# GpSimd's memsets between scatters: one of 192 floats behind each, or three of 336 behind two of thirteen

## The chip, the cores and the metric

One core of one Trainium2 chip. The metric is the time on the device in microseconds, median of several runs; lower is better. The engines are TensorE (PE in the profile, PEld for its weight loads), VectorE (DVE), ScalarE (ACT), GpSimd (POOL) and SyncE (SP). Transfers are issued from the queues of SyncE, ScalarE and GpSimd.

## The reference

A layer of a graph network: 6250 nodes with 64 features, 206,250 edges with 64 features.

```python
msg = concat([x[dst], edge_attr], axis=1)            # 206250 x 128
h = relu(msg @ W1a.T + b1a) @ W1b.T + b1b
sums = segment_sum(h, src, 6250)                     # counts likewise
agg = sums / max(counts, 1)[:, None]
z = relu(concat([x, agg], axis=1) @ W2a.T + b2a) @ W2b.T + b2b
out = layernorm(x + concat([z, x], axis=1) @ Wr.T + br)
```

The edges are ordered by `dst`; the sum is over `src`, whose values are spread over all nodes.

## The kernel before

`fast_path` does the work; `general_path` is taken only for inputs that it can't handle, and isn't run here. The edges are padded and cut into 124 blocks (`k`) of 13 tiles (`j`) of 128 edges. The bins of the sum are 49 groups of 128 nodes.

For each block:

- SyncE loads the block's edge features into `rhs` (L698, four buffers), the places of its `dst` nodes (L914), and the window of 64 node rows that they can lie in (L919).
- VectorE turns the places into a one-hot matrix below the features (`columns`, L931), and counts the edges of each bin (`bins_of`, L833 to L840); TensorE completes the counts (`counts_of`, L853 and L854), and VectorE makes of them the row in DRAM to which each edge goes (`slots`, L870 and L875).
- TensorE multiplies `rhs` by the first layer's weights (`hidden`, L951, two matmuls for each tile of edges), 4, 3, 3 and 3 tiles at a time, and ScalarE writes the relu of each part to the row buffer `orow` (L952). There are five such buffers. ScalarE also copies the node's place in its bin into each row (L1186). This copy is the first write to a buffer and waits until the 13 scatters that used the buffer five blocks earlier have landed.
- GpSimd scatters the 13 tiles (`scatter`, L958): 128 rows of 520 bytes each, to `rows` in DRAM, sorted by bin. Behind each scatter it sets the tile `rest` to zero (L966). Nothing reads `rest`.

Rows that are complete for a bin are read back by SyncE (`read`, L1008), VectorE makes a one-hot matrix of their nodes (L1034, L1037), TensorE sums them (`summed`, L1053), and the sums are added to `part` (L1107, L1109). These reads are spread over later blocks: an epoch's rows are read from four blocks after its end. What remains after the last block is read, summed and passed through the second layer and the normalisation (L1276 on).

The order on each engine is written out by hand: the loop over `k` emits for all engines in program order, and each engine takes its instructions in that order. On GpSimd that order is scatter, memset, scatter, memset. A scatter waits for the relu of its part and for the landing of the scatter eight before it. The memsets write the same tile, and in the built program each waits for the semaphore of the memset before it; a scatter doesn't wait for a memset.

Of the kernel before, what the change touches and what calls it, by code (L numbers as in the profile page):

```python
# [8 lines left out]
F32 = mybir.dt.float32  # L9
# [8 lines left out]
P = 128  # L18
# [446 lines left out]
SPREAD = 4.8  # L465
EARLY = 14
CLEAR = 4
FAR = -1000.0


# [7 lines left out]
def fast_path(  # L478
# [34 lines left out]
    nc = tc.nc  # L513
# [73 lines left out]
    const = ctx.enter_context(tc.tile_pool(name="fconst", bufs=1))  # L587
# [88 lines left out]
    with (  # L676
# [10 lines left out]
        slp = by_slot.enter_context(tc.tile_pool(name="slot", bufs=2))  # L687
        slp1 = by_slot.enter_context(tc.tile_pool(name="slot1", bufs=1))

        rest = const.tile([P, 192], F32, name="rest")  # L690
        orows = [op.tile([P, BLK, W], F32, name=f"orow{i}") for i in range(ROWS)]
        for r in orows:
            nc.gpsimd.memset(r[:, :, H], 1.0)
# [260 lines left out]
        def scatter(ep_, k):  # L954
            e, orow = epochs.index(ep_), orows[k % ROWS]
            for j in range(BLK):
                t = k * BLK + j
                s = nc.gpsimd.indirect_dma_start(  # L958
                    out=ep_.rows,
                    out_offset=bass.IndirectOffsetOnAxis(ap=rowidx[:, t : t + 1], axis=0),  # L960
                    in_=orow[:, j, :],
                    in_offset=None,
                )
                tc.declare_no_dep(s.ins, group=f"slots{e}", reason="each slot is written once")
                tc.add_to_no_dep_group(f"slots{e}", s.ins)
                nc.gpsimd.memset(rest, 0.0)  # L966
                tc.add_to_no_dep_group(f"block{k}", s.ins)
                scattered[t] = s.ins.name
                for i, st in enumerate(ep_.steps[:-1]):
                    if st.at <= k:  # L970
                        tc.declare_no_dep(s.ins, group=f"reads{i}", reason="later edges have later slots")
                if k < EARLY:
                    tc.declare_no_dep(s.ins, group="cleared", reason="no edge has these slots yet")
                if k == EARLY and j == 0:
                    for c in cleared:
                        tc.add_manual_dep(
                            s.ins, c.name,
                            mybir.DependencyInfo(mybir.DependencyClass.Sync, mybir.DependencyReason.DATA),
                            reason="edges may have these slots",
                        )  # L980
# [3 lines left out]
        def clear(e, i):  # L984

            ep_ = epochs[e]
            v = ep_.rows.rearrange("(b s) f -> b s f", b=NB)
            step = (NB - 1) // CLEAR
            parts = [(i * step, (i + 1) * step)] + [(NB - 1, NB)] * (i == CLEAR - 1)
            for b0, b1 in parts:  # L990
# [33 lines left out]
        def nodes_of(st, reads):  # L1024
# [3 lines left out]
            for b0, nb, t0, n, rt in reads:  # L1028
                node = rt[:, :, H + 1]
                if st is ep_.steps[-1] and t0 + n > ep_.low[b0]:  # L1030
# [3 lines left out]
                    nc.vector.scalar_tensor_tensor(  # L1034
                        node, ep_.unused[rest][:, at : at + nb * n], FAR, rt[:, :, H + 1], op0=ALU.mult, op1=ALU.add
                    )
# [101 lines left out]

        clears = {5 + 2 * i: (0, i) for i in range(CLEAR)}
        for e in range(1, BUFS):  # L1140
            clears.update({8 * e + 2 + 2 * i: (e, i) for i in range(CLEAR)})
        assert max(clears) < EPOCHS[0] and 5 + 2 * CLEAR <= EARLY

# [36 lines left out]
        for k, ep_ in enumerate(epoch_of):  # L1180
# [66 lines left out]
            for i in range(max(due, 1)):  # L1247
                if due > 0:
                    sum_next()
                    issue(k)  # L1250
                if i == 0 and k + 1 < NGR:
                    slots(k + 1, counts)
                if i == min(1, max(due, 1) - 1):
                    if k > 0:
                        hidden(k, ((10, 3),))
                    made.pop(k)
                    scatter(ep_, k)
# [179 lines left out]
```

## Time and profile before

| | |
|---|---|
| median of 3 runs | 2540.11 us (2535.44 to 2542.4) |
| the profiled execution | 2518.58 us |
| its span | 2516.8 us |
| mean granted TensorE clock | 0.687 |
| GpSimd busy | 2002.8 us (80%) |
| TensorE matmuls busy | 1581.3 us (63%) |
| VectorE busy | 1186.3 us (47%) |
| ScalarE busy | 331.3 us (13%) |

The profile is one execution. Each row of a group gives line, engine, operation, what is written from what is read, and the count, then busy time and the mean length of one in ns, then the engine's idle time ahead of these instructions and what ended it. "Issue" is idle time in which the engine waited for nothing that the profile shows; "remote" is a wait whose releaser it can't name. In a timeline row stand start and length in us, engine, line and operation; in brackets the idle time ahead of it. In a row of the windows stand the stretch, its length, the busy time of PE, PEld, DVE, ACT and POOL with counts, the granted clock, the mean busy share of the DMA engines, and GB/s.

### The profile page before, as it was taken

The numbers are of one execution on the slowest core, as the hardware profiler recorded it, in microseconds if no ns is written. First come the engines' busy times: TensorE is split into PE (matmuls) and PEld (weight loads), VectorE is DVE, ScalarE is ACT, GpSimd is POOL, SyncE is SP. The second block draws the span as 40 slices with busy tenths as digits, with TensorE's granted clock in tenths as the row PEclk, the third lists the DMA queues.
The fourth block names the chain that finished last, engine by engine and source line by source line (L and its number), as shares of the span: only waits on it lengthen the run. The fifth ranks groups of instructions, "written<-read, shape, count | busy, mean of one in ns | idle before, by whom it ended". The sixth has DMA issues, their size and how long they took to land.

```text
span 2516.8 us, 26639 instructions
## 1 busy us (share of the span) xinstructions
PE 1581.3 (63%) x8253; PEld 1341.0 (53%) x8253; DVE 1186.3 (47%) x1993; ACT 331.3 (13%) x807; POOL 2002.8 (80%) x3241
## 2 busy tenths in 40 slices
PE   3645543556656555565655676666766776767796
PEld 3634432444455445454444565565655565656695
DVE  5433442434344434353434454574545464546587
ACT  1211110101111111011111110111111110110115
POOL 7888888888888888888888888888878888888800
PEclk7666665656666676666666677676767676767798
DMA  6758554744454344344345454554545454446581
GB/s 165 215 178 280 157 157 119 204 116 116 116 143 133 105 133 122 111 130 116 116 118 142 128 168 145 159 167 137 165 121 167 147 176 145 151 149 182 168 259 36
DMA packets 198852, 375.33 MB, mean 149 GB/s; under 512 B 47106, under 2 KB 114037, under 8 KB 198573
## 3 DMA queue, kind: packets, MB, share of 16 engines
q1 hardware_dynamic: 121370, 223.70, 32.1%
q0 software_dynamic: 51584, 107.40, 13.4%
q10 hardware_dynamic: 25746, 42.45, 5.0%
q8 instruction: 67, 1.10, 0.2%
q14 instruction: 85, 0.69, 0.1%
HBM read 221.77 MB, written 151.59 MB: 148 GB/s over the span
## 4 chain that ended last, share of the span: by engine, by line
PE 31%; another core or an unknown queue 29%; issue 18%; DVE 10%; DMA 5%; SPq 5%; ACT 2%; ACTq 0%; DVEq 0%
PE sum_ps L1053 16%; PE h_ps L951 10%; DMA rt<-rows 3%; DVE oh L1037 2%; DVE rhs L931 2%; PE cnt_ps L853 1%; PE cnt_ps L854 1%; DVE had L840 1%; SPq L1008 1%; SPq L919 1%; DVE row L870 1%; SPq L914 1%; SPq L917 1%; PE h_ps L1162 1%
## 5 line engine op out<-in xcount | busy, mean ns | idle before, releaser
L958 POOL DMA_INDIRECT rows<-orow,rowidx x1612 | 1560.3, 968 | 390.5 <-issue 263.8
L951 PE MATMUL h_ps<-mv,rhs 128*128 128x128 f32 x3224 | 672.7, 359 | 371.6 <-issue 253.2
L1053 PE MATMUL sum_ps<-rt,oh 128*128 128x129 f32 x4006 | 720.5, 328 | 275.5 <-issue 253.3
L951 PEld LDWEIGHTS h_ps<-mv,rhs 128*128 128x128 f32 x3224 | 592.7, 263 | 462.1 <-issue 326.7
L1053 PEld LDWEIGHTS sum_ps<-rt,oh 128*128 128x128 f32 x4006 | 634.9, 235 | 346.5 <-issue 322.8
L952 ACT ACTIVATE orow<-h_ps 128x512 f32<-128x512 f32 x496 | 251.4, 518 | 2010.6 <-remote 1329.7
L966 POOL MEMSET rest<- 128x192 f32 x1612 | 443.4, 275 | 1.2
L1037 DVE TENSOR_TENSOR oh<-ramp,rt 128x512 f32<-128x512 f32 (+3 forms) x213 | 146.2, 703 | 560.8 <-DMA rt<-rows 369.4
L931 DVE TENSOR_TENSOR rhs<-rhs,ramp 64x1664 f32<-64x1664 bf16 x116 | 219.4, 1892 | 25.1 <-DMA rhs<-relt 14.2
L840 DVE TENSOR_TENSOR_SCAN had<-ramp,bins 128x700 bf16<-128x700 bf16 x124 | 200.3, 1615 | 4.2
L1109 DVE TENSOR_TENSOR part<-part,sum_ps 128x258 f32<-128x258 f32 (+2 forms) x183 | 86.1, 471 | 236.2 <-remote 160.2
L1037 DVE TENSOR_TENSOR oh<-ramp,node 128x512 f32<-128x512 f32 (+3 forms) x237 | 187.4, 791 | 8.0
L853 PE MATMUL cnt_ps<-had,one_w 128*128 128x350 bf16 x248 | 102.9, 417 | 118.5 <-issue 63.8
L870 DVE TENSOR_REDUCE row<-cnt_ps 128x14 f32<-128x700 f32 x124 | 109.0, 879 | 122.4 <-remote 98.9
L1034 DVE SCALAR_TENSOR_TENSOR node<-unused,rt 128x4 f32<-128x4 bf16 (+3 forms) x237 | 37.7, 159 | 171.6 <-DMA rt<-rows 132.3
L854 PE MATMUL cnt_ps<-bins,before_w 128*128 128x325 bf16 x248 | 104.4, 423 | 14.0 <-issue 13.2
L854 PEld LDWEIGHTS <-before_w 128*128 128x128 bf16 x248 | 29.4, 119 | 156.0 <-issue 143.2
L834 DVE TENSOR_TENSOR bins<-ramp,hi 128x650 bf16<-128x650 f32 x124 | 108.2, 873 | 0.0
L1158 DVE TENSOR_SCALAR zT<-h_ps 128x512 f32<-128x512 f32 (+1 forms) x13 | 8.6, 661 | 123.1 <-remote 107.9
L1162 PE MATMUL h_ps<-nwzz_t,zT 128*128 128x64 f32 x98 | 21.1, 385 | 63.3 <-DVE zT L1158 49.4
L1162 PEld LDWEIGHTS h_ps<-nwzz_t,zT 128*128 128x128 f32 x98 | 19.2, 291 | 65.0 <-issue 41.8
L853 PEld LDWEIGHTS <-one_w 128*128 128x128 bf16 x248 | 30.8, 124 | 30.3 <-issue 20.4
(113 smaller groups left out, 428.0 us busy)
## 6 DMA issues: line engine op xcount, KB each, us to landing
rt<-rows SPq DMA_DIRECT2D x242, 260.0 KB
rhs<-in_edgeT SPq DMA_DIRECT2D x124, 416.0 KB
rt<-rows SPq DMA_DIRECT2D x106, 390.0 KB
rows<-orow,rowidx POOLq DMA_INDIRECT x1612
rhs<-relt SPq DMA_DIRECT2D x116, 208.0 KB
rows<-padrow ACTq DMA_DIRECT2D x4, 4680.0 KB
rows<-padrow ACTq DMA_DIRECT2D x8, 2340.0 KB
rt<-rows SPq DMA_DIRECT2D x48, 325.0 KB
```

What stands on the lines that cost most here:

```text
L834: nc.vector.tensor_tensor(by_bin[:, :, 1:], ramp[:, : 2 * HALF, None].to_broadcast([P, 2 * HALF, BLK]), hi[:, None, c0 : c0 + BLK].to_broa ...
L840: nc.vector.tensor_tensor_scan(had, on, oh, 0.0, op0=ALU.mult, op1=ALU.add)
L853: nc.tensor.matmul(v, one_w, had[:, b, :], start=True, stop=False)
L854: nc.tensor.matmul(v[:, :, :BLK], before_w, oh[:, b, 1:], start=False, stop=True)
L870: nc.vector.tensor_reduce(row, v.rearrange("p i b t -> p t i b"), axis=mybir.AxisListType.XY, op=ALU.max)
L931: nc.vector.tensor_tensor(rhs[D:, :].rearrange("p (h e) -> p h e", h=2), rel, in_win[D:, :, None].to_broadcast([WIN, 2, NG * P // 2]), op= ...
L951: nc.tensor.matmul(ps[:, j, :], rhs[:, c * P : (c + 1) * P], m, start=True, stop=True)
L952: nc.scalar.activation(orow[:, k0 : k0 + n, :H], ps[:, :n, :], AF.Relu)
L958: s = nc.gpsimd.indirect_dma_start(out=ep_.rows, out_offset=bass.IndirectOffsetOnAxis(ap=rowidx[:, t : t + 1], axis=0), in_=orow[:, j, :], ...
L966: nc.gpsimd.memset(rest, 0.0)
L1037: nc.vector.tensor_tensor(res[:, at_tile : at_tile + nb * n, :], ramp[:, None, :].to_broadcast([P, nb * n, P]), node[:, :, None].to_broadc ...
L1053: nc.tensor.matmul(of_bin(b), oh[:, at_tile, :], rt[:, j * n + t, : H + 1], start=t0 + t == st.lo[b], stop=t0 + t == st.hi[b] - 1,)
```

## The change

The tile `rest` grows from 192 to 336 floats per partition. Behind the sixth and the thirteenth scatter of a block GpSimd sets all of it to zero three times; behind the other eleven it sets one float per partition to zero, once. The number of scatters, their order and their data stay the same, and so do the instructions of all other engines. The three memsets of a group write the same tile, and each waits for the semaphore of the one before it.

```diff
 CLEAR = 4
+REST = 336
+AT = (5, 12)
...
-        rest = const.tile([P, 192], F32, name="rest")
+        rest = const.tile([P, REST], F32, name="rest")
...
-                nc.gpsimd.memset(rest, 0.0)
+                for _ in range(3 if j in AT else 1):
+                    nc.gpsimd.memset(rest if j in AT else rest[:, :1], 0.0)
```

## The prediction

> **What bounds the kernel now.** I read the page first, for the busy shares and the chain that ended last; then GpSimd's groups by form and the waits; then the timeline at three places where GpSimd ran dry.
>
> ```profile
> span 2516.8 us, 26639 instructions
> PE 1581.3 (63%) x8253; PEld 1341.0 (53%) x8253; DVE 1186.3 (47%) x1993; ACT 331.3 (13%) x807; POOL 2002.8 (80%) x3241
> PE 31%; another core or an unknown queue 29%; issue 18%; DVE 10%; DMA 5%; SPq 5%; ACT 2%; ACTq 0%; DVEq 0%
> ...
> L958 POOL DMA_INDIRECT rows<-orow,rowidx x1612 | 1560.3, 968 | 390.5 <-issue 263.8 <-ACT orow L1186 64.7 <-ACT orow L952 61.4
> L966 POOL MEMSET rest<- 128x192 f32 x1612 | 443.4, 275 | 1.2
> ...
> 14.49 1.13 POOL L958 DMA_INDIRECT rows<-orow,rowidx  x1 [11.34 <-ACT orow L952]
> ...
> 2394.89 0.27 POOL L966 MEMSET rest<- 128x192 f32 x1
> ```
>
> The two GpSimd rows give busy time, mean length of one, and the idle time before them. Scatters 1560.3, memsets 443.4 and idle 390.5 + 1.2 add up to 2395 us, which is where GpSimd's last memset ends (2394.89 + 0.27 = 2395.2). So GpSimd is occupied or held from start to that point, and 121.6 us of tail follow without it. Of its idle time 263.8 us is the fixed gap ahead of a scatter (0.17 us each), and 64.7 + 61.4 = 126.1 us are waits for ScalarE's rows, 11.3 of them before the very first scatter. GpSimd alone would therefore need 2395.2 - 126.1 = 2269 us; it has 114.8 us of later waits in it, so it isn't the only bound.
>
> ```profile
> POOL rows L958 <- ACT orow L1186: 64.7, 26, 5.8
> POOL rows L958 <- ACT orow L952: 61.4, 35, 11.3
> ...
> ACT orow L952 <- remote: 1329.7, 177, 21.7
> ...
> ACT orow L1186 <- DMA rows<-orow,rowidx: 5.7, 1, 5.7
> ```
>
> The columns are total us, times, longest. ScalarE's relu L952 waits 1329.7 us for something that the profile can't name. What it needs is TensorE's products. It isn't short of row buffers: the copy L1186, the instruction that must wait until the scatters of five blocks earlier have landed, waited once, for 5.7 us. So the side of TensorE and ScalarE isn't held back by GpSimd through the buffers, and yet it is as slow as GpSimd. The timeline shows how the two are tied:
>
> ```profile
> 639.04 0.97 POOL L958 DMA_INDIRECT rows<-orow,rowidx  x1 [0.16 <-issue]
> 641.80 0.48 SPq L698 DMA_DIRECT2D rhs<-in_edgeT  x1
> 641.87 0.49 ACT L952 ACTIVATE orow<-h_ps 128x384 f32<-128x384 f32 x1 [16.06 <-remote]
> 642.64 0.97 POOL L958 DMA_INDIRECT rows<-orow,rowidx  x1 [2.36 <-ACT orow L1186]
> ...
> 1166.64 0.37 PE L951 MATMUL h_ps<-mv,rhs 128*128 128x128 f32 x1 [1.02 <-issue]
> 1167.37 0.37 PE L951 MATMUL h_ps<-mv,rhs 128*128 128x128 f32 x1 [0.36 <-issue]
> 1169.56 0.96 POOL L958 DMA_INDIRECT rows<-orow,rowidx  x1 [0.16 <-issue]
> 1170.97 0.97 POOL L958 DMA_INDIRECT rows<-orow,rowidx  x1 [0.16 <-issue]
> 1173.77 0.48 SPq L698 DMA_DIRECT2D rhs<-in_edgeT  x1
> 1173.84 0.49 ACT L952 ACTIVATE orow<-h_ps 128x384 f32<-128x384 f32 x1 [16.48 <-remote]
> 1174.60 0.97 POOL L958 DMA_INDIRECT rows<-orow,rowidx  x1 [2.40 <-ACT orow L1186]
> 1175.82 3.51 PE L1053 MATMUL sum_ps<-rt,oh 128*128 128x129 f32 x24
> ...
> 2116.30 0.96 POOL L958 DMA_INDIRECT rows<-orow,rowidx  x1 [0.16 <-issue]
> 2119.09 0.49 SPq L698 DMA_DIRECT2D rhs<-in_edgeT  x1
> 2119.16 0.49 ACT L952 ACTIVATE orow<-h_ps 128x384 f32<-128x384 f32 x1 [19.56 <-remote]
> 2119.93 0.97 POOL L958 DMA_INDIRECT rows<-orow,rowidx  x1 [2.39 <-ACT orow L1186]
> ```
>
> Scatters follow each other every 1.41 us (1169.56, 1170.97). At 1166 us TensorE starts single matmuls 0.73 us apart, with idle time that nothing explains, and ScalarE stands still for 16.48 us. Then GpSimd runs out of rows and misses a slot, and SyncE, ScalarE and TensorE all start again: 24 matmuls in 3.51 us. Had the restart nothing to do with GpSimd, the time from the last scatter to it would be scattered over anything from 0 to 20 us. It is 2.76, 2.80 and 2.79 us in the three places, after ScalarE waits of 16 to 20 us, and GpSimd's own waits are 2.36, 2.40 and 2.39 us. I read this as: an unbroken train of scatters slows TensorE's side down, and a pause in the train of somewhere between 1.4 and 2.8 us, from one scatter's start, sets it free. What carries this I can't see. Two more rows speak for it:
>
> ```profile
> 467.00:2395.00 1928.00, 1249.38 (x6399) 1059.12 (x6398) 905.43 (x1406) 215.82 (x511) 1619.69 (x2614) 0.68 0.48 140
> 2395.00:2516.80 121.80, 97.76 (x723) 87.50 (x722) 98.47 (x348) 44.72 (x133) 0.17 (x1) 0.93 0.50 150
> ```
>
> After the last scatter TensorE does 723 matmuls in 121.8 us, 5.9 per us, at a granted clock of 0.93; beside the scatters 3.3 per us at 0.68. DMA is equally busy in both (0.48 and 0.50).
>
> **The change, part by part.** It touches GpSimd's memsets only; their order among the scatters stays, no other engine's instructions move, nobody reads what they write. A block has 13 scatters, so 11 memsets of 192 floats become one float, and two become three of 336. Over 124 blocks that is 1364 short and 744 long ones in place of 1612.
>
> ```profile
> L671 POOL MEMSET padrow<- 128x780 f32 x1 | 0.7, 739 | 0.0
> masks.py:197 POOL MEMSET ident<- 128x128 f32 x1 | 0.2, 195 | 0.0
> L1419 POOL MEMSET const-float32-1.0<- 128x1 f32 x1 | 0.1, 99 | 0.0
> ...
> 0.25 0.10 POOL L1419 MEMSET const-float32-0.0<- 128x1 f32 x1 [0.25 <-issue]
> 0.28 0.10 POOL L1419 MEMSET const-float32-1.0<- 128x1 f32 x1
> ...
> 1.30 0.52 POOL L648 MEMSET rt<- 65x512 f32 x1
> 1.76 0.20 POOL masks.py:197 MEMSET ident<- 128x128 f32 x1
> ```
>
> Price of a float: (739 - 195) / (780 - 128) = 0.834 ns. From L966's 275 ns at 192 floats: one float costs 275 - 191 x 0.834 = 116 ns (99 by the row of that size), 336 floats 275 + 144 x 0.834 = 395 ns. End to end: 1364 x 0.116 + 744 x 0.395 = 158.2 + 293.9 = 452.1 us against 443.4, so +9 us. The second and third long memset of a group have no row here. Below: independent memsets overlap (0.25 and 0.28; 1.30 + 0.52 against 1.76), by some 0.06 us; 496 of these save 30 us, and the 99 ns row saves 1364 x 0.017 = 23 us more, together 9 - 53 = -44 us. Above: all write the same tile, and each waits for the semaphore of the one before. From a relu's end (2119.16 + 0.49) to the scatter that waits for it (2119.93) it takes 0.28 us; 496 x 0.28 = 139, so +148 us. I take +9, since L966's row shows 1.2 us of idle time in 1612, so GpSimd takes up a ready memset at once, and keep -44 and +148 for the range.
>
> [...] The overlap is in the rows above for tiles that don't depend on each other. [...]
>
> What the change moves is where GpSimd pauses. Behind 11 scatters the next one starts 0.97 + 0.116 + 0.17 = 1.25 us later, behind the sixth and thirteenth 0.97 + 3 x 0.395 + 0.17 = 2.32 us later. Before, no stop was longer than 1.41 us unless GpSimd ran dry. 2.32 lies inside the 1.4 to 2.8 us above. If the pause frees TensorE's side, it does so 248 times, every 6 or 7 scatters, and GpSimd runs dry less often. Waits before a block's first scatter or its eleventh are the ones that it can shorten; I count half of the 114.8 us, since 2.32 falls short of the 2.8 us seen: -57 us. This half is an estimate between none and all. Sum: +9 - 57 = -48 us. The profiled execution took 2518.58 us; 2518.6 - 48 = 2470.6. The median of the runs, 2540.11, stands 0.85% above it, so 2470.6 x 1.0085 = 2492 us. GpSimd is then the bound of the scatter stage (2278 us of its own and some 69 us of waits), and the tail's 121.6 us stay. With all waits gone and the lower price it would be 2518.6 - 115 - 44 = 2360, or 2380 us on the median's scale.
>
> The granted clock may add to it: 0.68 beside the scatters against 0.93 in the tail. [...]
>
> **The rivals.** *A, the short gaps hurt (slower).* If TensorE's side advances only in the gap between two scatters, that gap falls from 0.275 + 0.17 = 0.45 us to 0.29 us behind 11 of 13 scatters, and stalls grow between the long pauses. It decides if 2.32 us is too short to set TensorE free. Every 5% on the 1329.7 us of ScalarE's waits is 66 us: 2518.6 + 9 + 66 = 2594, or 2616 us. For it: the releases seen came at 2.76 us and later. Against it: three places only, and the next scatter needs time to take hold.
>
> *B, GpSimd gets longer.* With 0.28 us at each of 496 semaphores GpSimd needs 2269 + 148 = 2417 us without any wait, 22 us past today's 2395, and some 10 us of waits remain: 2518.6 + 32 = 2551, or 2572 us. For it: the wait is in the built instruction list. Against it: both ends are the same engine, while the 0.28 us is between two.
>
> *C, nothing comes of it.* The pauses free nothing, and TensorE's side, which doesn't wait for GpSimd's buffers, keeps its pace; then +9 us or -44 us disappear into the 114.8 us of waits: 2540 us. For it: the L1186 row. Against it: the restarts above.
>
> That the change doesn't do what it says is ruled out by the instruction list: one-float memsets behind 11 scatters, three of 336 behind the sixth and thirteenth.
>
> **How the numbers follow.** Forecast 0.54, A 0.18, B 0.16, C 0.12. About 0.3% (8 us) is what a measurement of this kernel can tell from no change, so faster 0.54, same 0.12, slower 0.34. The likeliest case's own range is 2380 to 2530; the range for 8 in 10 runs from 2410, which leaves out the extreme of full release with the lower price, to 2590, which takes in C, B and the start of A.
>
> **What would show it.** Right: L958's waits for ScalarE fall from 126 to near 70 us; L952's "remote" total falls well below 1329.7; ScalarE restarts in the pauses behind the sixth and thirteenth scatter; the long memsets follow each other 0.4 us apart. Wrong: the memsets stand 0.6 us or more apart (B); "remote" grows and GpSimd's waits with it (A); both stay (C).

## The result, and the profile after

The changed kernel took 2529.89 us (median of 13 runs, 2522.59 to 2534.48) against 2541.85 us for the kernel before in the same session (13 runs, 2535.44 to 2548.92). The medians lie 12 us apart, where 48 us were forecast. The ratio of the two, taken over all runs, is 0.9945 with a 95% interval of [0.9934, 0.9957], so the gain is about 0.5%. The profiled execution took 2527.26 us, span 2525.5 us.

GpSimd's groups by form in the profile after, then its waits and ScalarE's (total us, times, longest). The added lines shift the numbers: scatter L960, memset L969, relu L954, copy L1189, sums L1056.

```profile
L960 POOL DMA_INDIRECT rows<-orow,rowidx x1612 | 1551.4, 962 | 376.3 <-issue 324.8 <-ACT orow L954 25.3 <-ACT orow L1189 11.8
L969 POOL MEMSET rest<- 128x336 f32 x744 | 286.8, 385 | 28.7
L969 POOL MEMSET rest<- 128x1 f32 x1364 | 160.4, 118 | 0.5
...
POOL rows L960 <- issue: 324.8, 1575, 2.0
POOL rows L960 <- ACT orow L954: 25.3, 23, 3.3
POOL rows L960 <- ACT orow L1189: 11.8, 8, 2.1
...
ACT orow L954 <- remote: 1146.7, 205, 18.5
...
ACT orow L1189 <- DMA rows<-orow,rowidx: 203.4, 27, 14.8
```

GpSimd's waits for ScalarE's rows fell from 126.1 to 37.1 us, and the copy into a row buffer now waits 203.4 us for scatters to land, against 5.7 us before: in places GpSimd has become the slower side. But the gap that the profile calls "issue" rose from 263.8 to 324.8 us, and 28.7 us of idle time stand ahead of the long memsets. The timeline shows where they come from:

```profile
1008.09 0.96 POOL L960 DMA_INDIRECT rows<-orow,rowidx  x1 [0.19 <-issue]
1009.04 1.27 POOL L969 MEMSET rest<- 128x336 f32 x3
1010.67 0.97 POOL L960 DMA_INDIRECT rows<-orow,rowidx  x1 [0.36 <-issue]
1011.64 0.11 POOL L969 MEMSET rest<- 128x1 f32 x1
1011.95 0.96 POOL L960 DMA_INDIRECT rows<-orow,rowidx  x1 [0.19 <-issue]
...
1017.01 0.96 POOL L960 DMA_INDIRECT rows<-orow,rowidx  x1 [0.19 <-issue]
1017.95 1.27 POOL L969 MEMSET rest<- 128x336 f32 x3
1019.39 0.98 POOL L960 DMA_INDIRECT rows<-orow,rowidx  x1 [0.16 <-issue]
```

A one-float memset is followed by a gap of 0.19 us instead of 0.16; the first scatter of a block, behind three long memsets, comes after 0.36 us; and three memsets of 0.385 us take 1.27 us, so 0.058 us lies between two (28.7 us over 496). The stop behind the sixth scatter is 2.38 us from start to start (1017.01 to 1019.39), that behind the thirteenth 2.58 us (1008.09 to 1010.67).

The same two kernels ran once more in another session, the second of those below: 2544.95 us before, 2530.92 after, ratio 0.9945 [0.9925, 0.9965]. Its rows, before and after:

```profile
L958 POOL DMA_INDIRECT rows<-orow,rowidx x1612 | 1557.0, 966 | 421.6 <-issue 265.3 <-ACT orow L952 72.6 <-ACT orow L1186 67.8
L966 POOL MEMSET rest<- 128x192 f32 x1612 | 442.4, 274 | 1.0
```

```profile
L960 POOL DMA_INDIRECT rows<-orow,rowidx x1612 | 1547.2, 960 | 388.7 <-issue 325.1 <-ACT orow L954 30.5 <-ACT orow L1189 18.8
L969 POOL MEMSET rest<- 128x336 f32 x744 | 285.5, 384 | 28.6
L969 POOL MEMSET rest<- 128x1 f32 x1364 | 158.3, 116 | 1.0
```

Put into a ledger, which adds up to GpSimd's end, with the tail as what is left of the span:

| us | before | after | before, 2nd session | after, 2nd session |
|---|---|---|---|---|
| scatters | 1560.3 | 1551.4 | 1557.0 | 1547.2 |
| memsets | 443.4 | 447.2 | 442.4 | 443.8 |
| idle ahead of memsets | 1.2 | 29.2 | 1.0 | 29.6 |
| "issue" ahead of scatters | 263.8 | 324.8 | 265.3 | 325.1 |
| GpSimd's own total | 2268.7 | 2352.6 | 2265.7 | 2345.7 |
| other idle time ahead of scatters | 126.7 | 51.5 | 156.3 | 63.6 |
| tail | 121.4 | 121.4 | 124.5 | 119.8 |
| span | 2516.8 | 2525.5 | 2546.5 | 2529.1 |

GpSimd's own total grew by 84 and 80 us; its waits shrank by 75 and 93 us. Two large terms nearly cancel. The first pair of profiled executions even comes out 9 us slower. The profiled execution before (2518.58 us) isn't one of the 13 runs and lies 17 us under the fastest of them, and the record names no chip for it, so this pair may mix two chips. The second pair (17 us faster) is from one chip and lies near its medians (14 us faster); it is the one to go by.

### The profile page after: what moved, and what is told of

It reads as the page before. It is cut to its first block, busy times and chain, and to the rows that moved or that the text cites. A ratio compares the mean times of both kernels' runs of the same rounds, so it can differ in the third digit from the quotient of the medians.

```text
span 2525.5 us, 27135 instructions
## 1 busy us (share of the span) xinstructions
PE 1627.6 (64%) x8253; PEld 1402.9 (56%) x8253; DVE 1189.2 (47%) x1993; ACT 332.2 (13%) x807; POOL 1994.9 (79%) x3737
## 4 chain that ended last, share of the span: by engine, by line
PE 34%; another core or an unknown queue 23%; issue 17%; POOL 9%; DVE 8%; DMA 3%; SPq 3%; ACT 2%; ACTq 0%; POOLq 0%; DVEq 0%
PE sum_ps L1056 17%; PE h_ps L953 13%; POOL rows L960 7%; POOL rest L969 2%; DMA rt<-rows 2%; DVE oh L1040 2%; ACT orow L954 1%; PE cnt_ps L855 1%; PE cnt_ps L856 1%; DVE rhs L933 1%; DVE had L842 1%; SPq L1011 1%; PE h_ps L1165 1%; DVE part L1112 1%
## 5 line engine op out<-in xcount | busy, mean ns | idle before, releaser
L960 POOL DMA_INDIRECT rows<-orow,rowidx x1612 | 1551.4, 962 | 376.3 <-issue 324.8
L953 PE MATMUL h_ps<-mv,rhs 128*128 128x128 f32 x3224 | 702.6, 372 | 444.6 <-issue 240.9
L953 PEld LDWEIGHTS h_ps<-mv,rhs 128*128 128x128 f32 x3224 | 620.1, 274 | 537.9 <-issue 311.4
L1056 PE MATMUL sum_ps<-rt,oh 128*128 128x129 f32 x4006 | 728.5, 338 | 235.3 <-issue 199.8
L1056 PEld LDWEIGHTS sum_ps<-rt,oh 128*128 128x128 f32 x4006 | 662.0, 247 | 288.5 <-issue 253.1
L954 ACT ACTIVATE orow<-h_ps 128x512 f32<-128x512 f32 x496 | 250.9, 518 | 1808.4 <-remote 1146.7
L969 POOL MEMSET rest<- 128x1 f32 (+1 forms) x2108 | 447.2, 212 | 29.2
L1189 ACT CAST orow<-lo 128x13 f32<-128x13 bf16 x124 | 25.9, 209 | 220.9 <-DMA rows<-orow,rowidx 203.4
```

The source lines that it names most:

```text
L953: nc.tensor.matmul(ps[:, j, :], rhs[:, c * P : (c + 1) * P], m, start=True, stop=True)
L954: nc.scalar.activation(orow[:, k0 : k0 + n, :H], ps[:, :n, :], AF.Relu)
L960: s = nc.gpsimd.indirect_dma_start(out=ep_.rows, out_offset=bass.IndirectOffsetOnAxis(ap=rowidx[:, t : t + 1], axis=0), in_=orow[:, j, :], ...
L969: nc.gpsimd.memset(rest if j in AT else rest[:, :1], 0.0)
L1056: nc.tensor.matmul(of_bin(b), oh[:, at_tile, :], rt[:, j * n + t, : H + 1], start=t0 + t == st.lo[b], stop=t0 + t == st.hi[b] - 1,)
```

## The experiments

The kernel before does not take the same time on all chips, and neither do the others in proportion to it. In two sessions it took 2378.52 and 2378.86 us, in four others 2514.66, 2515.93, 2544.95 and 2541.85 us (the last is the session of the result). All kernels of one session share a chip, and each ratio is against the kernel before on that chip. The five sessions below ran on five different chips; for the session of the result the chip isn't on record. Each chip was used in one session only, so a property of the chip can't be told from one of the session. I call the chips of the first two quick and the others slow. Unless shown otherwise an edit is made to the changed kernel.

The theories: the **pause theory** is the prediction's (a stop in the train of scatters sets TensorE's side free). Against it stands the **pace** or **total theory**: only GpSimd's own total counts, wherever its slack stands. Rival A of the prediction (short gaps hurt) can act beside either.

### First session, a quick chip (before 2378.52 us)

**No pause**: one float behind every scatter. **One pause**: `AT = (12,)`. **Half pause**: one long memset instead of three. **Even**: 250 floats behind every scatter.

```diff
 e1_no_pause
-                for _ in range(3 if j in AT else 1):
-                    nc.gpsimd.memset(rest if j in AT else rest[:, :1], 0.0)
+                nc.gpsimd.memset(rest[:, :1], 0.0)
 e2_one_pause
-AT = (5, 12)
+AT = (12,)
 e3_half_pause
-                for _ in range(3 if j in AT else 1):
+                for _ in range(1):
 e4_even
-REST = 336
+REST = 250
...
-                for _ in range(3 if j in AT else 1):
-                    nc.gpsimd.memset(rest if j in AT else rest[:, :1], 0.0)
+                nc.gpsimd.memset(rest, 0.0)
```

> One float is set behind every scatter; no long memset is left. GpSimd's own cycle is then 1.27 us for each scatter, 2041 us over the kernel (2342 us in the changed kernel). Pause theory (an unbroken train of scatters slows TensorE's side, a stop of some 2.4 us frees it): the stops are gone, so TensorE's side falls back, GpSimd waits for rows for over 300 us in all, and the time is that of the kernel before or longer, 2540 to 2600 us. Pace theory (only GpSimd's own total counts, wherever it stops): 300 us less of its own, so 2400 to 2500 us.

> The three memsets of 336 floats stay behind the thirteenth scatter alone; one float behind the other twelve. GpSimd's own cycle is 12 x 1.27 + 2.59 = 17.8 us per block, 2205 us in all. Pause theory: half as many stops, so stalls grow up to a block's length and GpSimd's waits rise to 150 us or more; 2530 to 2560 us. Pace theory: 137 us less than the changed kernel, so 2480 to 2520 us.

> One memset of 336 floats behind the sixth and thirteenth scatter in place of three: the stop is 1.52 us from scatter to scatter in place of 2.4 to 2.6. GpSimd's own cycle is 17.0 us per block, 2104 us in all. Pause theory: 1.52 us is too short to free TensorE's side, so it comes out as with no stops, 2540 to 2600 us. Pace theory: 240 us less of its own than in the changed kernel, so 2430 to 2500 us.

> One memset of 250 floats behind every scatter: a scatter every 1.45 us, 18.9 us per block, the same own total as in the changed kernel (2342 us), spread evenly. Pause theory: no stop, so stalls of over 10 us stay, and GpSimd's longer own time comes on top of what its waits can take in: 2540 to 2590 us. Pace theory: the same total, so the changed kernel's time, about 2530 us.

Measured: no pause 2156.47 us, ratio 0.9065 [0.9053, 0.9078]; one pause 2322.61, 0.9763 [0.9750, 0.9777]; half pause 2218.57, 0.9330 [0.9318, 0.9343]; even 2454.00, 1.0319 [1.0305, 1.0334]. All the ranges that were expected, in both theories, stood on a kernel before of 2540 us, and all are missed. The differences fit the pace theory: against the changed kernel's 2462.66 us on a quick chip (fourth session) these four are 306, 140, 244 and 9 us faster, where GpSimd's own totals were expected 301, 137, 238 and 0 us shorter. ScalarE's two largest waits in the kernel without a pause:

```profile
ACT orow L1188 <- DMA rows<-orow,rowidx: 1459.0, 111, 15.4
ACT orow L954 <- PE h_ps L953: 184.3, 153, 6.8
```

No "remote" wait of the relu is left. The copy waits 1459 us for scatters to land, so TensorE's side is the full five buffers ahead at 111 of 124 blocks, with no pause in the train at all. On this chip nothing has to be set free: the pause theory fails here, and so does A.

### Second session, a slow chip (before 2544.95 us)

> The changed kernel itself, unedited, beside the kernel before in the same runs. Pace theory (where TensorE is not stalled, the time is GpSimd's own total and nothing else): the pauses cost 79 us of GpSimd's own time (2342 against 2263 us in the first pair of traces), so where the kernel before takes 2378 us the changed one takes about 2457 us, ratio 1.033. Pause theory (a stop behind the sixth and thirteenth scatter frees TensorE's side): a gain wherever it runs, ratio 0.98 to 0.995. Where the kernel before takes 2540 us again, both give 2530 us, ratio 0.995.

> The kernel before, unedited, for a trace beside the others. Where it takes 2378 us: pace theory expects that ScalarE's relu has next to no waits that the profile can't name (under 100 us against 1329.7 in the first trace) and that the copy waits for the landing of scatters of five blocks earlier instead, some 1600 us. Pause theory expects the unnamed waits of 16 to 20 us to be there still, some 1300 us in sum. Where it takes 2540 us, both expect the first trace again.

> One float behind every scatter, no pause at all. Pace theory: GpSimd's own total falls by about 225 us to 2035 us; where the kernel before takes 2378 us this takes 2157 us, ratio 0.907; where it takes 2540 us, TensorE's side is the limit and the time lies between 2300 and 2540 us, ratio 0.91 to 1.00. Pause theory: a train without a pause of over 0.29 us stalls TensorE's side more often, so where the kernel before takes 2540 us this is slower than the changed kernel, above 2530 us and up to 2616 us.

> 250 floats behind every scatter: GpSimd's own total is about that of the changed kernel (2336 against 2342 us), spread evenly, cadence 1.45 us, no pause. Pace theory: the time of the changed kernel within 0.5%: 2454 us where the kernel before takes 2378 us, ratio 1.032; about 2530 us where it takes 2540 us. Pause theory: where the kernel before takes 2540 us, this one keeps the stalls and has 73 us more of GpSimd's own time, 2580 to 2620 us, ratio 1.015 to 1.03, clearly slower than the changed kernel.

Here g3_short is the kernel without a pause, and g4_even the one with 250 floats. Measured: the changed kernel 2530.92 us, 0.9945 [0.9925, 0.9965]; the kernel before 0.9998 [0.9981, 1.0016]; short 2585.98, 1.0150 [1.0127, 1.0174]; even 2525.31, 0.9916 [0.9896, 0.9935]. The kernel that won 9.3% on the quick chip loses 1.5% here, and the one that lost 3.2% wins 0.8%. GpSimd's groups and ScalarE's longest wait of short, then of even:

```profile
L960 POOL DMA_INDIRECT rows<-orow,rowidx x1612 | 1546.0, 959 | 727.3 <-issue 298.6 <-ACT orow L954 224.3 <-ACT orow L1188 190.6
L968 POOL MEMSET rest<- 128x1 f32 x1612 | 189.5, 118 | 3.4 <-remote 1.4 <-POOL rest L968 1.3
...
ACT orow L954 <- remote: 1259.2, 113, 23.2
```

```profile
L960 POOL DMA_INDIRECT rows<-orow,rowidx x1612 | 1557.5, 966 | 321.5 <-issue 261.3 <-ACT orow L954 30.9 <-ACT orow L1188 16.6
L968 POOL MEMSET rest<- 128x250 f32 x1612 | 522.0, 324 | 1.0
...
ACT orow L954 <- remote: 1421.4, 236, 19.9
```

Short has 228 us less of its own than the kernel before (1546.0 + 298.6 + 189.5 + 3.4 = 2037.5 against 2265.7), and waits 429 us (727.3 - 298.6) for rows in place of 156. GpSimd's end comes at 2466 us instead of 2422: with GpSimd out of the way sooner, TensorE's side has become slower. So on this chip denser scatters do slow it, which is rival A. Even has the changed kernel's own total (2342 against 2346) and no pause, and is not slower (the intervals overlap): against an even spread the two stops gain nothing.

The timeline of short shows one stall:

```profile
1018.57 3.10 PEld L953 LDWEIGHTS h_ps<-mv,rhs 128*128 128x128 f32 x14
1018.82 0.12 POOL L968 MEMSET rest<- 128x1 f32 x1
1018.86 3.01 PE L953 MATMUL h_ps<-mv,rhs 128*128 128x128 f32 x14
...
1022.92 0.96 POOL L960 DMA_INDIRECT rows<-orow,rowidx  x1 [0.19 <-issue]
1023.87 0.12 POOL L968 MEMSET rest<- 128x1 f32 x1
1026.43 0.49 SPq L700 DMA_DIRECT2D rhs<-in_edgeT  x1
1026.49 0.49 ACT L954 ACTIVATE orow<-h_ps 128x384 f32<-128x384 f32 x1 [15.82 <-remote]
1026.88 0.20 ACT L1188 CAST orow<-lo 128x13 f32<-128x13 bf16 x1
1026.97 0.98 ACT L954 ACTIVATE orow<-h_ps 128x512 f32<-128x512 f32 x2
1027.04 1.35 PEld L953 LDWEIGHTS h_ps<-mv,rhs 128*128 128x128 f32 x6 [5.36 <-ACT orow L954]
```

TensorE's 14 products end at 1021.87 us. ScalarE, idle since 1010.67, takes its next part at 1026.49, 3.57 us after the last scatter's start, and then three in a row without a wait; SyncE starts at the same moment. As far as the records show, the products were there 4.62 us before ScalarE went on (1026.49 - 1021.87); what held it and SyncE until then no row shows. I counted the waits of ScalarE's relu of more than 8 us between 467 and 2350 us, in the timeline. In the kernel before 42 of 93 (the profile of the prediction) and 39 of 89 (its trace beside these) end in a stop of the train, one of over 1.8 us from start to start, at a median of 2.6 and 2.7 us after the last scatter's start; in short 76 of 104 do, at a median of 3.8 us. These counts don't show that the stop released ScalarE. Of the 42 stops 39, and of the 76 stops 73, ended because GpSimd got the row from ScalarE that it had been waiting for, so ScalarE's restart had to come first, whatever brought it about. And a stop isn't needed: in even 76 of 91 such waits end without one.

### Third session, a slow chip (before 2515.93 us)

Two pairs that were to have equal totals. **One long**: six memsets of 288 floats behind the thirteenth scatter only, one stop of 3.69 us, against the changed kernel. **Even 144** against **one pause**.

```diff
 h2_one_long
-REST = 336
-AT = (5, 12)
+REST = 288
+AT = (12,)
...
-                for _ in range(3 if j in AT else 1):
+                for _ in range(6 if j in AT else 1):
 h3_even144: as e4_even, REST = 144
 h4_one_pause: as e2_one_pause
```

> The changed kernel again, as the mark for the three others. Where the kernel before takes about 2540 us: 2530 us, ratio 0.9945, in every theory. Where it takes 2378 us: GpSimd's own total decides, 2378.5 + 79 = 2457 us, ratio 1.033.

> One float behind twelve scatters of a block, six times 288 floats behind the thirteenth: GpSimd's own total is the changed kernel's (about 2340 us), in one stop of 3.7 us instead of two of 2.4 us. Total theory (only GpSimd's own total counts, wherever the stops stand): the changed kernel's time within 0.4%, so ratio 0.991 to 0.999 where the kernel before takes 2540 us. Pause theory (each stop sets TensorE's side free once): half as many releases, so half of what the pauses gave is lost, 2545 to 2570 us, ratio 1.000 to 1.010. Where the kernel before takes 2378 us both give about 2458 us, ratio 1.033.

> 144 floats behind every scatter, cadence 1.364 us, GpSimd's own total 2197 us, no pause. Total theory, where the kernel before takes 2540 us: between the short (2586 us at 2057) and the kernel before (2545 at 2259), about 2558 us, ratio 1.005, since TensorE's side loses more the denser the scatters are. Pause theory: slower than the next run, which has the same total and a pause, by 15 us or more. Where the kernel before takes 2378 us: 2378.5 - 61 = 2317 us, ratio 0.974.

> Three times 336 floats behind the thirteenth scatter alone, one float behind the others: GpSimd's own total 2197 us, as with 144 floats everywhere. Total theory, where the kernel before takes 2540 us: the same as with 144 floats everywhere within 0.4%, about 2558 us, ratio 1.005. Pause theory: one release per block more than without a pause, so faster than 144 floats everywhere by 15 us or more, 2530 to 2545 us. Where the kernel before takes 2378 us: 2322 us, ratio 0.976.

Measured: the changed kernel 2504.29 us, 0.9954 [0.9938, 0.9971]; one long 2514.02, 0.9996 [0.9981, 1.0012]; even 144 2534.03, 1.0082 [1.0061, 1.0104]; one pause 2587.53, 1.0289 [1.0265, 1.0313]. GpSimd's scatters in even 144, then in one pause:

```profile
L960 POOL DMA_INDIRECT rows<-orow,rowidx x1612 | 1556.3, 965 | 469.1 <-issue 265.5 <-ACT orow L1188 103.3 <-ACT orow L954 87.4
```

```profile
L960 POOL DMA_INDIRECT rows<-orow,rowidx x1612 | 1550.7, 962 | 581.4 <-issue 316.6 <-ACT orow L1189 159.5 <-ACT orow L954 105.2
```

One pause was to be 15 us faster than even 144 by the pause theory, and equal by the total theory. It is 53.5 us slower: GpSimd waits 265 us in place of 191 for rows (159.5 + 105.2 and 103.3 + 87.4). Both theories fall in their plain form. Twelve short gaps in a row cost more than a stop of 2.58 us returns. Gathering the changed kernel's two stops into one costs 0.4% as well, as the pause theory expected (ratio 1.000 to 1.010) and the total theory did not (0.991 to 0.999); GpSimd's own total in the two traces is 2357 us with two stops and 2338 with one.

One long's trace says more on what a stop does, since its stops are built in and mostly don't wait for a row:

```profile
1420.25 0.96 POOL L960 DMA_INDIRECT rows<-orow,rowidx  x1 [0.53 <-issue]
1421.21 2.33 POOL L969 MEMSET rest<- 128x288 f32 x6
...
1423.53 0.49 SPq L700 DMA_DIRECT2D rhs<-in_edgeT  x1
1423.60 0.49 ACT L954 ACTIVATE orow<-h_ps 128x384 f32<-128x384 f32 x1 [15.13 <-remote]
...
1423.95 0.96 POOL L960 DMA_INDIRECT rows<-orow,rowidx  x1 [0.41 <-issue]
```

ScalarE and SyncE start 3.3 us after the thirteenth scatter's start, and the next scatter follows at GpSimd's own pace. Counted as above, 47 of 61 long waits end in a stop, at a median of 3.5 us after the scatter's start, though such stops are 21% of the time; 33 of the 47 stops ended without a wait for a row. In the changed kernel, with stops of 2.38 and 2.58 us, 19 of 72 (the profile after) and 32 of 98 (second session) do, and such stops are 28 and 29% of the time: no more than by chance. Just around the end of these stops, 2 to 4 us after the sixth or thirteenth scatter's start, which is a fifth of the time, more of them end, 28 of 72 and 38 of 98; but in the kernel before, which has no stop built in there, 30 of 93 and 30 of 89 do. So restarts gather in a stop of 3.69 us, and for the shorter ones that isn't shown. Every engine repeats its work with the block, so a fixed place in the block could put the restarts there too; no run parts the two.

### Fourth session, a quick chip (before 2378.86 us), and fifth, a slow one (before 2514.66 us)

**Three**: `AT = (3, 8, 12)` and two long memsets instead of three, stops of 1.95 to 2.15 us. Half pause is that of the first session.

> The changed kernel as the mark for the three others. Where the kernel before takes 2510 to 2550 us: ratio 0.9945 to 0.9955, as in the runs so far. Where it takes 2378 us: 2457 us, ratio 1.033, by GpSimd's own total.

> One float behind every scatter again, beside the two that follow. Where the kernel before takes 2510 to 2550 us: ratio 1.015, as measured once; a stop removed from the changed kernel costs TensorE's side more than GpSimd gains. Where it takes 2378 us: 2157 us, ratio 0.907.

> The changed kernel's two stops cut to one memset of 336 floats each, so 1.52 us from scatter to scatter instead of 2.4 and 2.6. Where the kernel before takes 2510 to 2550 us: if any stop past 1.4 us sets TensorE's side free, as the prediction bounded it, most of the gain stays, ratio 0.985 to 1.000. If the length of the stop counts, 0.25 us more is next to nothing and the short gaps' loss stays: ratio 1.010 to 1.030. Where it takes 2378 us: 2219 us, ratio 0.933.

> Two times 336 floats behind the fourth, ninth and thirteenth scatter, one float behind the others: three stops of about 1.95 us, trains of three to four short gaps, GpSimd's own total about 2310 us. Where the kernel before takes 2510 to 2550 us: if shorter trains help at this total, ratio 0.985 to 0.994, at or below the changed kernel; if the length of each stop counts more, 1.000 to 1.015. Where it takes 2378 us: 2378.5 + 50 = 2430 us, ratio 1.02.

> The two stops cut to 1.52 us from scatter to scatter. Where the kernel before takes 2378 us: 2219 us, ratio 0.933, by GpSimd's own total, as twice measured. Where it takes 2510 to 2550 us: if any stop past 1.4 us sets TensorE's side free, ratio 0.985 to 1.000; if the length of the stop counts, the loss of the short gaps stays, ratio 1.010 to 1.030.

> Three stops of about 2 us a block, one float elsewhere. Where the kernel before takes 2378 us: 2466 us, ratio 1.037, as measured once. Where it takes 2510 to 2550 us: if shorter trains help, ratio 0.985 to 0.994; if the length of each stop counts more, 1.000 to 1.015.

Measured on the quick chip: changed 2462.66 us, 1.0351 [1.0334, 1.0368]; short 2156.04, 0.9065 [0.9050, 0.9080]; half pause 2219.02, 0.9330 [0.9314, 0.9345]; three 2465.72, 1.0367 [1.0349, 1.0384] (1.02 was expected, from an own total of 2310 us; the trace has 2363). On the slow one: half pause 2560.88, 1.0177 [1.0151, 1.0202]; three 2488.89, 0.9899 [0.9871, 0.9927]. The changed kernel on the quick chip, its chain of waits, GpSimd's groups and ScalarE's waits:

```profile
POOL 70%; issue 13%; DMA 6%; DVE 5%; PE 3%; ACT 1%; SPq 1%; POOLq 0%; ACTq 0%; DVEq 0%
...
L960 POOL DMA_INDIRECT rows<-orow,rowidx x1612 | 1551.3, 962 | 355.6 <-issue 331.6 <-DVE rhs L928 11.6 <-ACT orow L1189 7.9
L969 POOL MEMSET rest<- 128x336 f32 x744 | 286.1, 385 | 28.7
...
ACT orow L1189 <- DMA rows<-orow,rowidx: 1768.2, 115, 18.3
ACT orow L954 <- PE h_ps L953: 181.1, 143, 6.8
```

The chain is GpSimd, 70%, and ScalarE waits for scatters to land. **So the change itself is 3.5% slower there**: its cost in GpSimd's own time is paid in full and there is no wait to save.

Half pause says that a stop of 1.52 us returns nothing that shows on a slow chip; its 1.0177 is no better than the 1.0150 of no pause (two chips, so which of them is worse isn't known). The rival expectation, that any stop past 1.4 us frees TensorE's side, is out. Three, with a train of three or four short gaps, leaves GpSimd next to no waits: ScalarE's waits and GpSimd's, on the slow chip:

```profile
ACT orow L1189 <- DMA rows<-orow,rowidx: 1042.1, 73, 18.5
ACT orow L954 <- remote: 470.1, 85, 16.9
...
POOL rows L960 <- DVE rhs L928: 11.2, 1, 11.2
POOL rows L960 <- ACT orow L954: 4.3, 5, 3.3
```

All kernels together. The slot is the interval from one scatter's start to the next without waits: the median at each of the 13 places of a block, in the timeline, averaged over the 13 (for 1 float from the quick chips, where no place has waits in its median).

| behind the scatters | slot, us | quick chips | slow chips |
|---|---|---|---|
| 1 float everywhere | 1.26 | 0.9065, 0.9065 | 1.0150 |
| 336 behind two, else 1 | 1.30 | 0.9330, 0.9330 | 1.0177 |
| 144 everywhere | 1.36 | | 1.0082 |
| 3 x 336 behind one, else 1 | 1.36 to 1.37 | 0.9763 | 1.0289 |
| 192 everywhere (before) | 1.40 | 1 | 1 |
| 6 x 288 behind one, else 1 | 1.45 | | 0.9996 |
| 3 x 336 behind two, else 1 (changed) | 1.45 | 1.0351 | 0.9945, 0.9945, 0.9954 |
| 250 everywhere | 1.45 | 1.0319 | 0.9916 |
| 2 x 336 behind three, else 1 | 1.45 | 1.0367 | 0.9899 |

On the quick chips the slot is the whole story: 2378.5 + 1611 x (slot - 1.403) (1.403 us is the slot before in the slow chips' traces) gives 2153, 2217, 2316, 2454 and 2461 us for slots of 1.263, 1.303, 1.364, 1.450 (even) and 1.454 (changed), against 2156, 2219, 2323, 2454 and 2463 measured; three, 2454 and 2466, is the furthest off. On the slow chips every kernel with a shorter slot than before is slower, those with a slot of 1.45 us are faster or equal, and at one slot the spread counts: one lump is worst in both groups where it was tried. No version is best on both kinds: 1 float everywhere is it by far on the quick chips, and 1.5% slower than before on a slow one; three stops have the lowest ratio on a slow one (another chip than even's and the changed kernel's, so their order isn't settled) and are 3.7% slower on a quick one.

What delays TensorE's side on the slow chips stays open. Every trace of a slow chip has it (470 to 1421 us of "remote" waits of the relu), none of a quick one. For one kernel (half pause) the stretch of 467 to 2050 us, in which both still scatter, on a quick and on a slow chip (PE, PEld, DVE, ACT, POOL with counts, clock, DMA share, GB/s):

```profile
467.00:2050.00 1583.00, 914.57 (x6032) 853.98 (x6032) 853.94 (x1317) 185.15 (x476) 1346.29 (x2415) 0.75 0.54 160
```

```profile
467.00:2050.00 1583.00, 868.20 (x4913) 767.48 (x4911) 719.77 (x1051) 173.25 (x425) 1177.42 (x2113) 0.71 0.48 134
```

On the slow chip TensorE gets 19% fewer matmuls through and GpSimd 13% fewer instructions, and less data is moved; all fall behind together, so these rows don't say what holds the others. Slower transfers aren't seen: in short the packets of GpSimd's scatters took 13.1% of 2584.9 us on the slow chip and 16.1% of 2154.1 on the quick one, 339 and 347 us, and those of the busiest queue 814 and 778 us. A test with scatters of half the data, which would have parted the transfers from GpSimd's part in them, wasn't tried: rows in DRAM would have been read unwritten.

## Why the prediction was right or wrong, point by point

- **Reading of the kernel before.** That GpSimd alone needed 2269 us and that TensorE's side was slowed while scatters ran holds for the slow chips (short is slower there with GpSimd sooner out of the way). The three restarts that were read as releases couldn't show one: the rows have GpSimd's next scatter waiting for ScalarE (`<-ACT orow L1186`), so each of those stops ended because ScalarE had restarted. And the kernel doesn't behave so everywhere: on the quick chips TensorE's side has no such stall, and GpSimd alone is the bound.
- **Price of a float**: right. 118 and 385 ns measured for 116 and 395; memsets +4 and +1 us (two pairs) for +9.
- **GpSimd's own total, +9 us: the step that failed.** It measured +84 and +80. On a quick chip the change costs just that, 84 us. The two terms left out are the gap ahead of a scatter, taken as a constant 0.17 us (0.19 behind one float, 0.36 at a block's first: 324.8 - 263.8 = +61 us), and the space between two long memsets, taken as nothing from a row in which no memset followed another (0.058 us, 496 times: +28 us with the 0.5 ahead of the short ones, against 1.2). The upper bound of +148 us held both. The lower one, -44 us, took 30 us from an overlap that memsets of one tile don't show: 0.058 us lies between two, and that isn't the 0.28 us of rival B either.
- **Waits, -57 us**: right in sign, under-sized. They fell by 75 and 93 us. With the two measured terms the sum is 2518.6 + 83.9 - 75.2 = 2527.3, the profiled execution's 2527.26; the tail is the same in both, so this is bookkeeping, and no test of why the waits fell. The granted clock, which the prediction thought might add to the gain and gave no term, was 0.70 beside the scatters (467 to 2395 us) in the profile after against 0.68, and 0.68 in both kernels of the second session (467 to 2350 us); what it did to the time no run shows.
- **Why they fell**: not shown to be the stops. The prediction put it all down to them, and set the shortened gaps at nothing. On a slow chip the shortened gaps alone cost 1.5% (short), and the two stops, put into that kernel, bring it from 1.0150 to 0.9945, 55 us (2585.98 to 2530.92). So rival A's loss is there, and the added slack first repays it. That the slack must stand in stops, which was the forecast's mechanism, isn't borne out: an even spread of it does as well (even), and the changed kernel's long waits end in its stops no more often than by chance (19 of 72 and 32 of 98). How much of the 75 to 93 us is due to wider spacing and how much only to GpSimd's longer own time taking up waits stays open.
- **The bound on the stop, 1.4 to 2.8 us.** The lower end was the interval of the train, the upper three restarts of one kernel, picked where GpSimd had run dry; over half of the long waits (51 of 93) end without a stop. 1.52 us gives nothing back that shows, one stop of 2.58 us per block doesn't pay for twelve short gaps, and the one stop in which restarts gather is 3.69 us long, with the restarts at a median of 3.5 us. So behind short gaps both of the change's stops, 2.38 and 2.58 us, look too short, which is the condition that the prediction gave for rival A.
- **The scale, 0.85%.** The profiled execution before had 126.7 us of waits, the one with a span of 2546.5 us in the second session 156.3, at nearly the same own total and tail. By these two, what lies between that profile and a median near 2540 us is more of the very waits that the change removes, and not a factor on the whole. Whether that holds for the session of the result isn't shown: no trace on record is known to be of the kernel before in it.
- **Rivals.** A: that the next scatter needs time to take hold, said against it, was the author's estimate; no run shows it. B: 0.058 us lay between two memsets of one tile, where 0.28 was feared for the semaphore wait. C: the time is nearly unchanged, but since two terms cancel, not since nothing happened. Slower, which was given 0.34, came true on a quick chip by rival B's way, GpSimd getting longer, but not at its price: the time lies in the gaps, and there are no waits for it to disappear into.
- **What would show it**: the waits for ScalarE fell below the 70 us expected (37.1), and long memsets start 0.44 us apart (0.385 + 0.058). ScalarE's restarts in the two stops, the sign that the mechanism hung on, are no more than the stops' share of the time. The relu's "remote" total fell only to 1146.7, and it is no measure of success: even has 1421.4 and is as quick.

## What to carry to other kernels

Before costing a filler on an engine's queue, count the gaps around it as well as its length: here all of the added time (61 + 28 of 84 us, the rest cancels) lay in gaps that changed with the instruction ahead of them. Before reading a pause as what set another engine free, check whether the pause ended because that engine had started again. Where one engine's train seems to slow another, vary the spacing evenly before shaping it into pauses, and try the kernel without any filler. And run such a tuned kernel on more than one chip: this change is 0.5% faster in three sessions on slow chips and 3.5% slower on a quick one, and the filler that it rearranges costs 9% on the quick ones.

## What the runs showed of the hardware that was not expected

The same kernel took 2378.5 to 2378.9 us in two sessions and 2515 to 2545 us in four, each steady within 1% and five of the six on chips known to differ, and most of the order of the variants is reversed between them. On the slow ones ScalarE's relu stands in waits that the profile can't name (470 to 1421 us in a trace, up to 28.5 us at a time); on the quick ones none occur. In one long, ScalarE's long waits end 3.5 us (median) after the start of the last scatter before a stop of 3.69 us; in even, with a scatter every 1.45 us, most end without a stop. A scatter's start comes 0.19 us behind a one-float memset, and 0.16 to 0.17 us behind a single one of 144 to 336; behind three of 336 it comes after 0.16 us in one place of the block and after 0.36 in another.
